# A conditioned residual layer on one core: b2's rows spread by TensorE, six of them behind the first up-projections, and the early loads reordered

## Chip, cores and metric

The kernel runs on one core of a Trainium2 chip. The metric is the device time of one launch in microseconds (us). Engines are named as the profile names them: PE (TensorE), DVE (VectorE), ACT (ScalarE), POOL (GpSimd) and SP (SyncE, which only issues DMAs here).

## What is computed

Each of 128 batches is a tile of 128 x 512 floats with an id (`itok`, 0 to 9 once clamped), which picks one of ten sets of weights.

```python
w1 = W1[language_ids]                       # 512 x 128
w2 = W2[language_ids]                       # 128 x 512
h = relu(einsum('bsh,bha->bsa', x, w1) + b1[language_ids][:, None, :])
adapted = einsum('bsa,bah->bsh', h, w2) + b2[language_ids][:, None, :]
y = x + adapted
normed = (y - mean(y)) * rsqrt(var(y) + 1e-5)          # over the last axis
return x + normed * gamma[language_ids][:, None, :] + beta[language_ids][:, None, :]
```

x and the output are 33.5 MB each, W1 and W2 2.6 MB each; beta, gamma, b2 are ten rows of 512.

## The kernel before

A batch is one tile: its 128 rows lie on the 128 partitions. Four batches make a group, which is one x tile (`xs[g]`, four buffers, 1 MB by one DMA in the loop; the first groups come in halves by `load_part`). The order on each engine is written out by hand: `keep` binds every instruction behind the one before it on its engine, so the order of the Python statements is the order of each queue. Waits between engines are placed by the framework from the data and from the buffers of the pools. A DMA also waits for the eighth DMA before it: there are eight completion semaphores in turn.

The work of one batch b, with its names:

- PE: `transpose_x` (four 128x128 transposes of x into PSUM, pxT), `down` (x times W1, ph: eight matmul records), `up` (hT times W2, py: two records; where `b2_by_matmul(b)` holds, a bf16 matmul with `pick` as weights adds b2's row to py first).
- ACT: `copy_xT` (pxT to SBUF), `relu` (ph to hT, with b1), `square` (sum of squares), for every second batch `deviation` (square root), and `stage_w1` (copies the id's W1 out of a resident copy into the buffer w1s).
- DVE: `residual` (py plus x, or plus r = x + b2, with the row's sum), `scale` (by gamma), `finish` (by the row's rstd, plus o), small statistics in between (`rstd_1` to `rstd_4`).
- POOL: `add_b2` (r = x + b2's spread row, where neither PE nor DVE adds b2) and `add_beta` (o = x + beta's spread row).
- SP: loads of x and the `store` of every second batch.

In iteration i of the loop PE does `transpose_x(i)`, `down(i-1)` and `up(i-2)`, and DVE and ACT finish batch i-3 and what is behind it. py has five PSUM buffers (`p_y`), pxT, ph and the statistics one each (`p_x`, `p_h`, `p_s`), w1s five SBUF buffers (`wp`).

Ahead of the loop the rows of beta, gamma and b2 have to stand on all 128 partitions, because the loop adds them by id. beta and gamma: the rows are split into three bf16 parts (`parts`), and `spread(r)` makes row r by one bf16 matmul with a one-hot `pick` into a py buffer, from which ACT (r % 3 == 1) or DVE copies it to `beta_b` or `gamma_b`. `spread_turn` puts these between the first transposes and downs; there are 20. b2 is loaded as one row into one partition (`b2_row`, inside the w1 tile, which is not yet in use), and POOL spreads it by three `partition_broadcast`. The downs of batches 0 to 3 stand ahead of the loop, and `up(0)`, `up(1)` behind them; `up(2)` and `up(3)` are in iterations 4 and 5.

W1 comes in three ways. For the first FIRST = 8 batches `load_first(b)` loads the id's W1 from DRAM straight into w1s[b]; SP reads the id into a register for that, and each load from the sixth on waits for the `down` that frees its buffer. Batches FIRST to 27 take W1 from `w1e`, a copy loaded by two `load_early` DMAs of 1.25 MB. From batch EARLY = 28 on they take it from `w1`, loaded by four `load_w1` inside the loop.

Of the kernel before, what the change touches and what calls it, by code (L numbers as in the profile page):

```python
# [8 lines left out]
FP = mybir.dt.float32  # L9
# [7 lines left out]
P = 128  # L17
G = 4
EPS = 1e-5
FIRST = 8  # L20
EARLY = 28
U = 2

# [2 lines left out]
def cond_resid_kernel(ctx: ExitStack, tc: tile.TileContext, x, itok, W1, b1, W2, b2, gamma, beta, out):  # L26
# [8 lines left out]
    nc = tc.nc  # L35
    B, S, H = x.shape
    L, _, A = W1.shape
# [7 lines left out]
    def keep(ins):  # L45

        engine = ins.ins.engine
        if engine in last:
            tc.add_manual_dep(ins.ins, last[engine], behind, reason="kept order")
        last[engine] = ins.ins.name  # L50
        return ins

    const = ctx.enter_context(tc.tile_pool(name="const", bufs=1))
    xp = ctx.enter_context(tc.tile_pool(name="xp", bufs=4))
# [7 lines left out]
    p_s = ctx.enter_context(tc.tile_pool(name="p_s", bufs=1, space=PSUM))  # L62
    p_y = ctx.enter_context(tc.tile_pool(name="p_y", bufs=5, space=PSUM))

    xs = {}

    def load_x(g):
        t = xp.tile([P, G, H], FP, tag="x", name=f"x_{g}")
        keep(nc.sync.dma_start(out=t, in_=x[g * G : (g + 1) * G].rearrange("b s h -> s b h")))
        xs[g] = t  # L70

    def xb(b):
        return xs[b // G][:, b % G, :]
# [5 lines left out]
    w1 = const.tile([P, L, KC, A], FP, name="w1")  # L79
# [5 lines left out]
    def load_part(lo, hi):  # L85
        dst = xs[lo // G][:, lo % G : lo % G + hi - lo, :]
        keep(nc.sync.dma_start(out=dst, in_=x[lo:hi].rearrange("b s h -> s b h")))  # L87
# [5 lines left out]
    load_part(0, 2)  # L93
    keep(nc.scalar.dma_start(out=b1r, in_=b1))

    b2_row = w1.rearrange("p l k a -> p (l k a)")[0:1, :]
    keep(nc.scalar.dma_start(out=b2_row, in_=b2.rearrange("(o l) h -> o (l h)", o=1)))

    warm = const.tile([P, 1], FP, name="warm")
    keep(nc.vector.memset(warm, 1.0))  # L100
    keep(nc.scalar.activation(warm, warm, AF.Sqrt))
    def load_w1(k):
        keep(
            nc.sync.dma_start(out=w1[:, :, k, :], in_=W1[:, k * P : (k + 1) * P, :].rearrange("l p a -> p l a"))
        )
# [46 lines left out]
    def load_first(b):  # L152
        w1s[b] = wp.tile([P, KC, A], FP, tag="w1s", name=f"w1s_{b}")
        src = W1[bass.ds(lid(b, ET.SP), 1)].rearrange("o (p k) a -> p (o k a)", k=KC)
        keep(nc.sync.dma_start(out=w1s[b].rearrange("p k a -> p (k a)"), in_=src))  # L155

    def load_w2(lo, hi):
        dst = w2[:, lo * H : hi * H].rearrange("p (l h) -> p l h", l=hi - lo)
        keep(nc.sync.dma_start(out=dst, in_=W2[lo:hi].rearrange("l a h -> a l h")))  # L159

    def load_early(lo, hi):
        dst = w1e[:, lo:hi].rearrange("p l k a -> p l (k a)")
        keep(nc.sync.dma_start(out=dst, in_=W1[lo:hi].rearrange("l (p k) a -> p l (k a)", k=KC)))

    load_w2(0, 2)
    load_first(0)
    load_first(1)
    load_part(2, G)
    load_first(2)
    load_first(3)  # L170
    load_w2(2, 6)
    load_w2(6, L)
    xs[1] = xp.tile([P, G, H], FP, tag="x", name="x_1")
    for b in (G, G + 2):
        load_part(b, b + 2)
        load_first(b)
        load_first(b + 1)
    xs[2] = xp.tile([P, G, H], FP, tag="x", name="x_2")
    load_part(2 * G, 2 * G + 2)
    load_early(0, 5)  # L180
    load_early(5, L)
    load_part(2 * G + 2, 3 * G)

    left = rp.tile([P, H], FP, tag="r", name="left")
    keep(nc.vector.tensor_copy(parts[0:R, :], rows[0:R, :]))
# [13 lines left out]
    beta_b = const.tile([P, L * H], FP, name="beta_b")  # L199
    gamma_b = const.tile([P, L * H], FP, name="gamma_b")  # L200
    b2_b = const.tile([P, L * H], FP, name="b2_b")
    for l in range(0, L, 4):
        span = slice(l * H, min(l + 4, L) * H)
        keep(nc.gpsimd.partition_broadcast(b2_b[:, span], b2_row[:, span]))  # L204

    def spread(r, copier):
        t = (beta_b, gamma_b)[r // L]
        row = p_y.tile([P, H], FP, tag="y", name=f"row_{r}")
        pick_r = pick[:, r : r + 1].to_broadcast([96, P])
        keep(nc.tensor.matmul(row, lhsT=pick_r, rhs=parts[:96, :], start=True, stop=True))  # L210
        dst = t[:, r % L * H : (r % L + 1) * H]
        if copier is nc.scalar:
            keep(nc.scalar.copy(dst, row))
        else:
            keep(nc.vector.tensor_copy(dst, row))  # L215
# [2 lines left out]
    phs, pxs, sums = {}, {}, {}  # L218

    def b2_by_matmul(b):  # L220
        return b < 4 or (b % 4 == 1 and not b2_by_vector(b))

    def b2_by_vector(b):
        return b % 8 == 5 and 8 <= b < B - 16
# [6 lines left out]
    def transpose_x(b):  # L231
        pxs[b] = p_x.tile([P, KC, P], FP, tag="xT", name=f"pxT_{b}")
        for k in range(KC):
            if b < EARLY:
                cols = xb(b).rearrange("s (p k) -> s k p", k=KC)[:, k, :]
            else:
                cols = xb(b)[:, k * P : (k + 1) * P]
            keep(nc.tensor.transpose(pxs[b][:, k, :], cols, ident))  # L238

    def copy_xT(b):  # L240
        xT[b] = tp.tile([P, KC, P], FP, tag="xT", name=f"xT_{b}")
        keep(nc.scalar.copy(xT[b], pxs.pop(b)))  # L242
# [14 lines left out]
    def down(b):  # L257
        phs[b] = p_h.tile([P, P], FP, tag="h", name=f"ph_{b}")
        for k in range(KC):
            keep(  # L260
                nc.tensor.matmul(  # L261
                    phs[b], lhsT=w1s[b][:, k, :], rhs=xT[b][:, k, :], start=(k == 0), stop=(k == KC - 1)
                )
            )
        del xT[b], w1s[b]
# [5 lines left out]
    def up(b):  # L271
        v = lid(b, ET.PE)
        ys[b] = p_y.tile([P, H], FP, tag="y", name=f"py_{b}")
        m = b2_by_matmul(b)
        if m:
            pick_b = pick[:, bass.ds(v + 2 * L, 1)].to_broadcast([96, P])
            keep(nc.tensor.matmul(ys[b], lhsT=pick_b, rhs=parts[:96, :], start=True, stop=False))  # L277
        keep(nc.tensor.matmul(ys[b], lhsT=hT[b], rhs=w2[:, bass.ds(v * H, H)], start=not m, stop=True))  # L278
        del hT[b]
# [78 lines left out]
    def on(b):  # L358
        return 0 <= b < B
# [123 lines left out]
    def spread_turn(lo, hi):  # L483
        for r in range(lo, hi):
            spread(r, nc.scalar if r % 3 == 1 else nc.vector)
# [9 lines left out]
    for b in range(4):  # L495
        down(b)
        if b < 2:
            transpose_x(b + 2)
        relu(b)
        if b < 2:  # L500
            copy_xT(b + 2)
        spread_turn((10, 14, 18, 20)[b], (14, 18, 20, 20)[b])
    up(0)
    up(1)

    for i in range(3, B + U):
        b = i - U - 1
        if b > G and b % G == 2 and b // G + 3 < NG:
            load_x(b // G + 3)
        if i == 5:  # L510
            load_x(3)
        if i in (8, 10, 12, 14):
            load_w1((i - 8) // 2)
        if i == 4:
            up(2)
        if i == 5:
            up(3)
        if i > 3 and on(i):
            transpose_x(i)
        if b <= E:  # L520
            add_b2(b + 2)
            add_beta(b)
        if i > 4 and on(i - 1):
            down(i - 1)
        if i > 3 and on(i):
            copy_xT(i)
        if i > 4 and on(i - 1):
            relu(i - 1)
        if i > 5 and on(i - U):
            up(i - U)  # L530


        g, half = divmod(b, 2)
        p = g - 1
        mine, old = 0 <= p < B // 2, 0 <= p - 1 < B // 2
        if b == E:
            add_b2(b + 3)
            add_beta(b + 1)
            add_b2(b + 4)
            for n in range(b + 2, B):  # L540
                add_beta(n)
        if b > E:
            tail(b)
        elif half == 0:
            if on(b):
                residual(b)
            if mine:
                rstd_1(p)
                scale(2 * p)
            if on(b):  # L550
                negative_mean(b)
            if mine:
                rstd_2(p)
            if old:
                finish(2 * p - 1)
                store(p - 1)
            if mine:
                rstd_3(p)
        else:
            if on(b):  # L560
                residual(b)
            if mine:
                rstd_4(p)
                scale(2 * p + 1)
            if on(b):
                negative_mean(b)
            if mine:
                finish(2 * p)
        if 0 <= b <= E:
            square(b)  # L570
            if half == 1:
                deviation(g)
        if i + 1 >= FIRST and on(i + 1):
            stage_w1(i + 1)

        for n, engine in ((i + 3, ET.Activation), (i - U + 3, ET.PE), (b + 1, ET.DVE), (b + 5, ET.Pool)):
            if on(n):
                lid(n, engine)
# [37 lines left out]
```

## Time and profile before

| what | value |
|---|---|
| median of three runs | 313.11 us (312.94 to 313.24) |
| profiled execution: its own time, and the span of its records | 312.74 us, 311.0 us |
| PE busy | 297.9 us, 96% of the span |
| DVE busy | 294.7 us, 95% |
| POOL busy | 285.4 us, 92% |
| ACT busy | 277.8 us, 89% |
| granted PE clock, mean | 0.989 of full speed |
| HBM read, written | 43.60 MB, 33.55 MB: 248 GB/s over the span |
| chain of work that ended last | PE 83%, DMA 8%, DVE 4% |

The shares of busy time are near each other and say little of which engine sets the pace; the slices of the span and the chain of waits are read for that. A PE record is a pipelined matmul whose end is modelled, so distances between starts are used for PE, not durations. Line numbers are those of this kernel; in the changed one they are a few lines lower.

### The profile page before, as it was taken

What the parts mean: (1) busy time and instruction counts of PE and PEld (TensorE: products, weight loads), DVE (VectorE), ACT (ScalarE), POOL (GpSimd) and SP (SyncE); (2) the same over time, 40 slices, a digit from 0 to 9 for tenths busy, and PEclk for the clock granted to TensorE, in tenths of its full rate; (3) what the DMA queues carried; (4) which work ended last, traced back from release to release, by engine and by line L of the source; (5) the groups of instructions that cost most, each with busy time, mean ns of one, the idle gap of its engine ahead of it and who ended that gap; (6) DMA issues with size and microseconds to landing.
All of it is one profiled execution on the core that took longest, in us unless ns stands there. A gap on an engine that the chain in (4) does not pass through costs nothing.

```text
span 311.0 us, 7063 instructions
## 1 busy us (share of the span) xinstructions
PE 297.9 (96%) x1846; PEld 223.1 (72%) x1846; DVE 294.7 (95%) x941; ACT 277.8 (89%) x710; POOL 285.4 (92%) x237
## 2 busy tenths in 40 slices
PE   8998899999999999999999999999999999999970
PEld 3766677878777777777777777777777777777740
DVE  6845999999999999999999999999999999999995
ACT  2655899999999999999999999999999999999982
POOL 1606999999999999999999999999999999999974
PEclk9999999999999999999999999999999999999995
DMA  6999999876777757677866766577765767773234
GB/s 218 346 387 388 373 368 349 295 263 210 269 271 238 233 192 245 231 237 254 270 245 211 232 201 265 209 266 271 249 227 194 245 233 239 245 270 135 87 154 169
DMA packets 43499, 77.61 MB, mean 250 GB/s; under 512 B 1946, under 2 KB 7077, under 8 KB 43459
## 3 DMA queue, kind: packets, MB, share of 16 engines
q1 hardware_dynamic: 43398, 77.10, 71.8%
q8 instruction: 15, 0.25, 0.3%
q14 instruction: 24, 0.20, 0.2%
q10 hardware_dynamic: 62, 0.07, 0.1%
HBM read 43.60 MB, written 33.55 MB: 248 GB/s over the span
## 4 chain that ended last, share of the span: by engine, by line
PE 83%; DMA 8%; DVE 4%; SPq 1%; issue 1%; ACT 1%; DVEq 1%; POOL 0%; ACTq 0%; POOLq 0%
PE ph L261 33%; PE py L278 32%; PE pxT L238 17%; DMA w1e<-in_L_cond_W_dram 4%; DMA x<-in_x_dram 3%; PE py L277 1%; DVE py L293 1%; DVE py L342 1%; DVE o L351 1%; SPq L155 1%; ACT sq L386 0%; SPq L87 0%; DVEq L611 0%; SPq L159 0%; ACT n L402 0%
## 5 line engine op out<-in xcount | busy, mean ns | idle before, releaser
L255 POOL TENSOR_TENSOR o<-x,beta_b 128x512 f32<-128x512 f32 x128 | 163.2, 1290 | 9.4 <-ACT hT L269 9.4
L261 PE MATMUL ph<-xT,w1s 128*128 128x128 f32 x1024 | 135.5, 275 | 0.0
L278 PE MATMUL py<-w,hT 128*128 x256 | 131.2, 594 | 1.4 <-DVE o L351 1.3
L261 PEld LDWEIGHTS ph<-xT,w1s 128*128 128x128 f32 x1024 | 125.0, 192 | 1.5 <-ACT hT L269 0.8
L248 POOL TENSOR_TENSOR r<-x,b_b 128x512 f32<-128x512 f32 x93 | 120.0, 1291 | 0.0
L238 PEld LDWEIGHTS pxT<-ident,x 128*128 128x128 f32 x512 | 67.4, 154 | 65.4 <-issue 47.3
L342 DVE SCALAR_TENSOR_TENSOR py<-py,nmean,gamma_b 128x512 f32<-128x512 f32 x126 | 93.3, 740 | 0.0
L351 DVE SCALAR_TENSOR_TENSOR o<-py,rstd,o 128x512 f32<-128x512 f32 x122 | 90.7, 744 | 1.4 <-POOL o L255 1.4
L308 ACT ACTIVATE sq<-py,sum 128x512 f32<-128x512 f32 x124 | 84.9, 685 | 4.3 <-DVE py L293 4.3
L238 PE MATMUL pxT<-ident,x 128*128 128x128 f32 x512 | 78.1, 275 | 0.5 <-ACT xT L242 0.5
L242 ACT COPY xT<-pxT 128x512 f32<-128x512 f32 x128 | 75.0, 586 | 1.7 <-PE pxT L238 1.6
L293 DVE SCALAR_TENSOR_TENSOR py<-py,r 128x512 f32<-128x512 f32 x93 | 64.4, 692 | 2.5 <-POOL r L248 1.7
L229 ACT COPY w1s<-w 128x512 f32 x100 | 61.2, 612 | 0.0
L269 ACT ACTIVATE hT<-ph,b1T 128x128 f32<-128x128 f32 x128 | 47.1, 368 | 11.2 <-PE ph L261 7.4
L278 PEld LDWEIGHTS py<-w,hT 128*128 128x128 f32 x256 | 40.4, 192 | 4.7 <-issue 1.7
L293 DVE SCALAR_TENSOR_TENSOR py<-py,x 128x512 f32<-128x512 f32 x35 | 24.3, 695 | 3.3 <-PE py L278 2.7
L308 ACT ACTIVATION_READ_ACCUMULATOR sq<-py,sum 128x1 f32 x124 | 25.2, 203 | 0.0
L319 ACT ACTIVATE sd<-ssq,eps 128x2 f32<-128x2 f32 x62 | 18.3, 296 | 2.1
L299 DVE TENSOR_SCALAR nmean<-sum 128x1 f32<-128x1 f32 x128 | 19.3, 150 | 0.1
L325 DVE RECIPROCAL stat<-sd 128x2 f32<-128x2 f32 x62 | 12.8, 207 | 1.3 <-ACT sd L319 1.3
L204 POOL PARTITION_BROADCAST b_b<-w x3 | 5.6, 1968 | 9.0 <-DVE beta_b L215 9.0
L229 ACT COPY w1s<-w1e 128x512 f32 x20 | 12.2, 612 | 1.3 <-DMA w1e<-in_L_cond_W_dram 1.2
(55 smaller groups left out, 119.7 us busy)
## 6 DMA issues: line engine op xcount, KB each, us to landing
out_dram<-o SPq DMA_DIRECT2D x61, 512.0 KB, 3.6
x<-in_x_dram SPq DMA_DIRECT2D x29, 1024.0 KB, 6.4
x<-in_x_dram SPq DMA_DIRECT2D x6, 512.0 KB, 7.0
w1e<-in_L_cond_W_dram SPq DMA_DIRECT2D x2, 1280.0 KB, 13.4
w<-in_L_cond_W_dram SPq DMA_DIRECT2D x4, 640.0 KB
w1s<-in_L_cond_W_dram SPq DMA_DIRECT2D x8, 256.0 KB, 6.2
w<-in_L_cond_W_dram SPq DMA_DIRECT2D x2, 1024.0 KB
out_dram<-o SPq DMA_DIRECT2D x6, 256.0 KB, 2.0
```

Source lines behind the costliest of these rows:

```text
L229: keep(nc.scalar.copy(w1s[b].rearrange("p k a -> p (k a)"), src))
L238: keep(nc.tensor.transpose(pxs[b][:, k, :], cols, ident))
L242: keep(nc.scalar.copy(xT[b], pxs.pop(b)))
L248: keep(nc.gpsimd.tensor_tensor(rs[b], xb(b), b2_b[:, bass.ds(v * H, H)], ALU.add))
L255: keep(nc.gpsimd.tensor_tensor(os[g][:, j, :], xb(b), beta_b[:, bass.ds(v * H, H)], ALU.add))
L261: nc.tensor.matmul(phs[b], lhsT=w1s[b][:, k, :], rhs=xT[b][:, k, :], start=(k == 0), stop=(k == KC - 1))
L269: keep(nc.scalar.activation(hT[b], phs.pop(b), AF.Relu, bias=b1T[:, bass.ds(lid(b, ET.Activation), 1)]))
L278: keep(nc.tensor.matmul(ys[b], lhsT=hT[b], rhs=w2[:, bass.ds(v * H, H)], start=not m, stop=True))
L293: nc.vector.scalar_tensor_tensor(ys[b], ys[b], 1.0, r, ALU.mult, ALU.add, accum_out=col(sums, b))
L308: nc.scalar.activation(sq, ys[b], AF.Square, bias=col(sums, b), scale=-float(H), accum_out=col(ssqs, b))
L342: nc.vector.scalar_tensor_tensor(ys[b], ys[b], col(nmeans, b), gamma_b[:, bass.ds(v * H, H)], ALU.add, ALU.mult)
L351: nc.vector.scalar_tensor_tensor(o, ys.pop(b), rstds[g][:, j : j + 1], o, ALU.mult, ALU.add)
```

## The change

Four edits go together.

- b2's rows: `b2_row` and the three broadcasts on POOL are gone. `spread` handles rows 20 to 29 (b2) too. Rows 20 to 23 join the turns ahead of the loop, which hold 5, 4, 3 and 2 rows now instead of 4, 4, 2 and 0. The last six, 24 to 29, are `spread_late`: their PSUM tile comes from `p_s`, which has one buffer and is shared with the statistics, and ACT copies them all. They stand behind `up(0)`, `up(1)`, `up(2)`, `transpose_x(4)`, `up(3)` and `down(4)`.
- `b2_by_matmul` holds for b < 6 instead of b < 4; batch 5 was already among them, so batch 4 is the one that moves from POOL to PE.
- FIRST is 12: `load_first` also serves batches 8 to 11, and the first `stage_w1` is that of batch 12. The four `load_w1` go from iterations 8 to 14 to iterations 14 to 20.
- SP's order: W2 is loaded in parts of 4 and 6 ids instead of 2, 4 and 4; x of batches 4 to 11 stands ahead of W1's early copy, whose halves stand around `load_first(10)`, `load_first(11)` and x of batches 12 and 13; x of 12 to 15 comes in halves there and no longer in iteration 5.

```diff
--- before.py
+++ after.py
@@ -17,7 +17,7 @@
 P = 128
 G = 4
 EPS = 1e-5
-FIRST = 8
+FIRST = 12
 EARLY = 28
 U = 2
 
@@ -92,9 +92,6 @@
     keep(nc.scalar.dma_start(out=rows[2 * L : 3 * L, :], in_=b2))
     load_part(0, 2)
     keep(nc.scalar.dma_start(out=b1r, in_=b1))
-
-    b2_row = w1.rearrange("p l k a -> p (l k a)")[0:1, :]
-    keep(nc.scalar.dma_start(out=b2_row, in_=b2.rearrange("(o l) h -> o (l h)", o=1)))
 
     warm = const.tile([P, 1], FP, name="warm")
     keep(nc.vector.memset(warm, 1.0))
@@ -162,24 +159,26 @@
         dst = w1e[:, lo:hi].rearrange("p l k a -> p l (k a)")
         keep(nc.sync.dma_start(out=dst, in_=W1[lo:hi].rearrange("l (p k) a -> p l (k a)", k=KC)))
 
-    load_w2(0, 2)
+    load_w2(0, 4)
     load_first(0)
     load_first(1)
     load_part(2, G)
     load_first(2)
     load_first(3)
-    load_w2(2, 6)
-    load_w2(6, L)
-    xs[1] = xp.tile([P, G, H], FP, tag="x", name="x_1")
-    for b in (G, G + 2):
+    load_w2(4, L)
+    for g in range(1, 4):
+        xs[g] = xp.tile([P, G, H], FP, tag="x", name=f"x_{g}")
+    for b in range(G, 10, 2):
         load_part(b, b + 2)
         load_first(b)
         load_first(b + 1)
-    xs[2] = xp.tile([P, G, H], FP, tag="x", name="x_2")
-    load_part(2 * G, 2 * G + 2)
+    load_part(10, 12)
     load_early(0, 5)
+    load_first(10)
+    load_first(11)
+    load_part(12, 14)
     load_early(5, L)
-    load_part(2 * G + 2, 3 * G)
+    load_part(14, 16)
 
     left = rp.tile([P, H], FP, tag="r", name="left")
     keep(nc.vector.tensor_copy(parts[0:R, :], rows[0:R, :]))
@@ -199,13 +198,10 @@
     beta_b = const.tile([P, L * H], FP, name="beta_b")
     gamma_b = const.tile([P, L * H], FP, name="gamma_b")
     b2_b = const.tile([P, L * H], FP, name="b2_b")
-    for l in range(0, L, 4):
-        span = slice(l * H, min(l + 4, L) * H)
-        keep(nc.gpsimd.partition_broadcast(b2_b[:, span], b2_row[:, span]))
-
-    def spread(r, copier):
-        t = (beta_b, gamma_b)[r // L]
-        row = p_y.tile([P, H], FP, tag="y", name=f"row_{r}")
+
+    def spread(r, copier, late=False):
+        t = (beta_b, gamma_b, b2_b)[r // L]
+        row = (p_s if late else p_y).tile([P, H], FP, tag="s" if late else "y", name=f"row_{r}")
         pick_r = pick[:, r : r + 1].to_broadcast([96, P])
         keep(nc.tensor.matmul(row, lhsT=pick_r, rhs=parts[:96, :], start=True, stop=True))
         dst = t[:, r % L * H : (r % L + 1) * H]
@@ -218,7 +214,7 @@
     phs, pxs, sums = {}, {}, {}
 
     def b2_by_matmul(b):
-        return b < 4 or (b % 4 == 1 and not b2_by_vector(b))
+        return b < 6 or (b % 4 == 1 and not b2_by_vector(b))
 
     def b2_by_vector(b):
         return b % 8 == 5 and 8 <= b < B - 16
@@ -499,29 +495,40 @@
         relu(b)
         if b < 2:
             copy_xT(b + 2)
-        spread_turn((10, 14, 18, 20)[b], (14, 18, 20, 20)[b])
+        spread_turn((10, 15, 19, 22)[b], (15, 19, 22, 24)[b])
+
+
+    def spread_late(r):
+        spread(r, nc.scalar, late=True)
+
     up(0)
+    spread_late(24)
     up(1)
+    spread_late(25)
 
     for i in range(3, B + U):
         b = i - U - 1
         if b > G and b % G == 2 and b // G + 3 < NG:
             load_x(b // G + 3)
-        if i == 5:
-            load_x(3)
-        if i in (8, 10, 12, 14):
-            load_w1((i - 8) // 2)
+        if i in (14, 16, 18, 20):
+            load_w1((i - 14) // 2)
         if i == 4:
             up(2)
+            spread_late(26)
         if i == 5:
             up(3)
+            spread_late(28)
         if i > 3 and on(i):
             transpose_x(i)
+        if i == 4:
+            spread_late(27)
         if b <= E:
             add_b2(b + 2)
             add_beta(b)
         if i > 4 and on(i - 1):
             down(i - 1)
+        if i == 5:
+            spread_late(29)
         if i > 3 and on(i):
             copy_xT(i)
         if i > 4 and on(i - 1):
```

## The prediction

> **What bounds the kernel now.** I read the 40 slices first, to see where the kernel is not full.
>
> ```profile
> PE   8998899999999999999999999999999999999970
> DVE  6845999999999999999999999999999999999995
> POOL 1606999999999999999999999999999999999974
> DMA  6999999876777757677866766577765767773234
> ```
>
> A slice is 7.8 us. From the fifth slice on all four engines stand at nine tenths; only the first four have holes, and there DMA is full. The waits between 48 and 300 us show no engine held for more than 0.4 us. The chain of waits says which of the full engines sets the pace.
>
> ```profile
> 8.18 10.55 DMA x<-in_x_dram
> 18.74 13.36 DMA w1e<-in_L_cond_W_dram
> 32.72 0.59 ACT xT L242
> 33.36 0.74 PE pxT L238 x4
> 34.10 0.89 PE ph L261 x8
> 34.99 0.86 PE py L278 x2
> ```
>
> Columns: start, length, what. After 34 us the chain is PE alone: 0.89 (down) + 0.86 (up) + 0.47 (transposes) = 2.22 us a batch, and 0.22 more where b2 goes by matmul (py L277 at 39.32, L278 at 39.54). The down of batch 8 (ph8) starts at 33.94 and that of batch 12 (ph12) at 43.08. So the end follows the moment at which PE gets into step: **every us by which ph12 moves, the end moves**. Before 34 us the chain is a DMA: SP issued W1's early copy late and it landed at 32.10.
>
> The waits from 5 to 34 us, and POOL's order of time, show who held PE there.
>
> ```profile
> POOL o L255 <- ACT hT L269: 9.4, 1, 9.4
> POOL b_b L204 <- DVE beta_b L215: 9.0, 1, 9.0
> PE py L278 <- DVE o L351: 1.3, 1, 1.3
> ACT w1s L229 <- DMA w1e<-in_L_cond_W_dram: 1.2, 1, 1.2
> PE pxT L238 <- ACT xT L242: 0.5, 1, 0.5
> 10.65 5.64 POOL L204 PARTITION_BROADCAST b_b<-w  x3 [8.95 <-DVE beta_b L215]
> 25.69 2.50 POOL L255 TENSOR_TENSOR o<-x,beta_b 128x512 f32<-128x512 f32 x2 [9.39 <-ACT hT L269]
> ```
>
> POOL stands 9 us ahead of its three broadcasts and 9.4 us behind them. The releasers named are chance: add_beta(0) needs only x and beta_b, done by 11.7. Because o comes at 25.69, finish(0) and finish(1) are late, and with them the PSUM slots of py5 and py6; ACT stands for w1e and PE for xT behind it.
>
> **What the Trainium skill says.** "GPSIMD Engine Reference", 2.1 Instruction dispatch: the first call to freshly loaded GpSimd code pays a load of about 6 us that has no instruction of its own in the profile. The two silent gaps fit, but here they are 9.0 and 9.4 us. "DMA: Bandwidth & Descriptors", Anatomy of one DMA: about 2 us fixed, most of it completion. Here the W2 rest landed at 17.37 (SP's wait for w ends there), 0.8 us after the bandwidth view had summed up to its last byte (4.8 MB), so less shows in a full queue. "Perfetto Trace Analysis", Optimization Strategy: repeated gaps on the engine that should be full can mean too few PSUM buffers for the next tile; before, py5 and py6 wait so, and the change makes a new chain through a single PSUM buffer.
>
> **The change, by parts.**
>
> Removed: b2_row's DMA and POOL's broadcasts with both gaps. POOL can start add_beta at 11.7 and is never late again, so PE's waits for finish go: py5's 0.5 us (27.29 to 27.79) and py6's 1.5 (29.33 + 0.89 = 30.22 to 31.72). One POOL add (b = 4, 1.26 us) turns into a PE matmul of 0.22.
>
> FIRST 12: ACT asks for w1e only after sq of batch 8, so px9's 0.8 us and ph8's 0.1 behind the 32.10 landing go as well. Before, PE's work from py0 (17.46) to ph8 (33.94), 16.48 us, is 7 ups 6.02, 4 pick matmuls 0.88, 6 transposes 2.82, 4 downs 3.56 = 13.28; **3.2 us are waits** (px5 and ph5 0.3, the rest as above).
>
> Added before py0: four rows of b2. Rows leave PE every 0.22 us (four from 13.59, ph2 at 14.45). DVE gets two more copies at 0.62, ACT one at 0.5; both keep up (last row at about 17.4; DVE free for residual 0 by 18.6). Starting from px2 at 10.80 as before and laying 14 rows, 3 downs and px3 end to end: ph1 12.5, ph2 14.7, ph3 16.3, py0 **17.8** instead of 17.46. W2's rest is no later in bytes (4.5 MiB queued up to it in both; estimate 16.7 to 17.4), so it no longer holds py0.
>
> Added after py0: six late rows (24 to 29) and b = 4's pick, 7 x 0.22 = 1.54 us of PE. Their copies are all on ACT, and their PSUM pool has **one** buffer: row n+1 waits for the copy of row n, and the ACT order is sq0, row 26, row 27, xT4, sq1, sd0, row 28, row 29, xT5. Prices, all from before: row start to copy 0.42 (13.59 to 14.01), copy 0.59, next ACT instruction after 0.50 (21.27 to 21.75), sq to sd 0.85, sd to next 0.2, xT's end to the next transpose 0.24 with its weight load (21.86 to 22.10). From py0 = 17.80:
>
> - bm1 18.88, bm2 20.18, row 26 21.26, px4 21.48. Copy 26 from 21.68 to 22.27; row 27 at 22.32 instead of 21.95: wait 0.4.
> - Copy 27 22.74, xT4 23.24 to 23.83, px5 24.07 (PE free at 23.84: 0.2), ph4 24.54.
> - sq1 23.74, sd0 24.6, copy 28 24.8 to 25.4, row 29 25.43, copy 29 25.85, xT5 26.35 to 26.94, px6 27.18. PE was free at 25.65: **wait 1.5**.
> - ph5 27.65, pick and py4 to 29.62, px7, ph6 30.09, pick and py5, px8, ph7 32.53, py6, px9, ph8 34.75. DVE's rstd of batch 0 sits behind copy 29 in the same PSUM buffer (26.5), finish(0) ends near 29.6, before py5's pick at 31.0; finish(1) near 32.0, before py6 at 33.4. No wait.
>
> Sum from py0 to ph8: 13.28 + 1.54 + waits 2.1 = 16.95. So ph8 is at 34.75 against 33.94: +0.34 (py0) + 1.54 (work) - 1.1 (waits 3.2 to 2.1) = +0.8. From there to ph12 three plain batches and one with the pick, 9.10 as before (9.14): ph12 43.85 against 43.08, **+0.8 us**.
>
> SP's queue: load_first(9), (10), (11) each wait for the W1 slot of a down (4, 5, 6), and w1e's second half and the x loads stand behind them. Up to the load for batch 8, 7.7 MB are queued, which the bandwidth view of before reaches at 24 us: DMA runs dry there and starts again at 25.6. From w1s of batch 9 to w1e's second half are 4.46 MB. Before, 4.72 MB took the 13.36 us up to 32.10, 0.353 MB/us; so 12.6 us, landing near 39 to 40.5. ACT needs it at 41.2 (ph10 at 39.2 + 1.1, hT 0.25, sq 0.66). Before, ph8 followed the landing by 1.84; ph12 at 43.85 is touched from a landing at **42.0** on. The cover is 1.5 us or more.
>
> At nothing: store(0) stands behind these loads, but its o slot is next used by add_beta(10), which has about 9 us before finish(10); W1's four loads move to iterations 14 to 20 and are needed at 28 (some 15 us later); x loads keep seven iterations ahead. If DMA stayed full past 60 us, xT of batch 24 would be late next.
>
> The profiled execution: 312.74 with span 311.0, 0.37 under the median 313.11. I add the difference to the median: 313.11 + 0.8 = **313.9**.
>
> **Rivals.**
>
> *The late rows hide (faster).* If ACT gets round to each copy while PE has other work, PE's new waits shrink from 2.1 to about 0.3. Then -3.2 + 1.54 + 0.34 + 0.3 = -1.0: 312.1. It decides from new waits under 0.7 us on. For it: ACT is idle 42% of 5 to 34 us. Against: idle time doesn't help a serial chain of five copies, two squares and a single buffer, whose every length is measured.
>
> *W1's early copy is late again (slower).* SP's waits for downs leave DMA idle, and stores and x behind w1e share the engines. Landing at 43.5 gives ph12 at 45.3: +2.3, 315.4; at 44.5, 316.4. For it: w1e landed 2.0 us after its byte count before. Against: that lag is in the 0.353.
>
> *Nothing to see.* Loss and gain are of one size; 0.5 us less ACT chain or py0 at 17.5 gives +0.3 or less, 313.4.
>
> POOL loading code in spite of the change is excluded: no broadcast is left in its queue.
>
> **How the numbers follow.** A measurement of this kernel tells about 0.2%, 0.63 us, from no change (312.48 to 313.74). Likeliest, +0.8: own range +0.2 to +1.7 (py0 17.5 to 18.3, chain 0.3 either way), 0.54. Late rows hidden, 0.16. Early copy late, 0.14. Nothing to see, 0.16. Of the likeliest about a quarter lies within 0.2% as well, and 0.02 of the hidden case. So faster 0.14, same 0.30, slower 0.56. Range for 8 in 10: 312.2 to 315.6, leaving out the best of the first rival and the worst of the second.
>
> **What would show it.** Right: POOL's first add at about 12 us and no idle after; row 29's copy at about 26 with px6 behind it, PE idle 1.5 us there; ph8 near 34.7; w1e landed by 41 with no ACT wait; 2.22 us a batch after that. Wrong: px6 before 26 (the rows hide); an ACT wait for w1e or for w1s; py0 after 18.5; any PE wait after 45 us.

## The result, and the profile after

| | before | after |
|---|---|---|
| median (lowest to highest), 13 runs each | 313.12 us (312.67 to 314.6) | 314.02 us (313.83 to 314.29) |
| profiled execution: its time, its span | 312.74, 311.0 us | 314.04, 312.3 us |
| down of batch 8 (ph8), of batch 12 (ph12) | 33.94, 43.08 us | 35.49, 44.59 us |
| from ph12 to the end of the span | 267.9 us | 267.7 us |

The ratio is 1.0025 with a 95% interval of 1.0016 to 1.0035: the change costs 0.9 us. The forecast was 313.9. Some executions of the kernel before and of e8 below (34 of 143, and 11 of 22) had a granted clock of 0.982 to 0.987 and took more than 314 us, so e8's median of 313.69 lies between two groups, the lower of them at 312.29 to 313.32.

First the slices of the changed kernel's page (rows 2, each digit a slice of 7.8 us):

```profile
PE   7898999999999999999999999999999999999970
DVE  6774999999999999999999999999999999999995
POOL 1504978999999999999999999999999999999974
DMA  6994999998776657677765767688676767783244
```

From the eighth slice on PE, DVE and POOL stand at nine tenths as before; what has moved lies in the first 55 us. PE is fuller in the fifth slice and emptier in the first two, POOL still has its empty third slice, and DMA, which was full in the fourth, stands at 4 there.

The chain of waits of the changed kernel (start, length, what) shows what ended last on the way to 35 us ("..." marks lines left out):

```profile
4.49 6.86 DMA x<-in_x_dram
11.48 0.72 PE pxT L234 x4
...
18.67 0.86 PE py L274 x2
...
22.55 0.59 ACT b_b L209
23.19 0.38 PE row L206
...
26.86 0.30 ACTq L134
27.16 0.60 ACT xT L238
27.81 0.74 PE pxT L234 x4
```

W1's early copy, which held 13.36 us of the chain before, is gone from it. In its place stand a load of x (batches 2 and 3, asked for at 4.49 and landed at 11.35), a copy of a late b2 row by ACT, and ACT's copy xT of batch 5. The waits from 5 to 36 us of the changed kernel put numbers on them:

```profile
POOL r L244 <- ACT b_b L209: 11.1, 1, 11.1
DVE stat L321 <- ACT b_b L209: 4.2, 1, 4.2
PE pxT L234 <- ACT xT L238: 1.2, 1, 1.2
PE pxT L234 <- DMA x<-in_x_dram: 1.0, 1, 1.0
```

The last two hold PE: 1.0 us at px2 (the transposes of batch 2) and 1.2 us at px6. The first two look large and cost nothing. DVE's reciprocal for batch 0 sits behind copy 29 in the same PSUM buffer and is still early enough. POOL, in its order of time:

```profile
11.31 4.96 POOL L251 TENSOR_TENSOR o<-x,beta_b 128x512 f32<-128x512 f32 x4 [9.85 <-DVE beta_b L211]
27.34 1.28 POOL L244 TENSOR_TENSOR r<-x,b_b 128x512 f32<-128x512 f32 x1 [11.08 <-ACT b_b L209]
```

It makes o for the first four batches at once, then stands until row 29 is copied, since r of batch 6 may be of any id. No PE wait follows from that.

### The profile page after: what moved, and what is told of

Same layout as the page of the kernel before. It is cut to its first block, busy times and chain, and to the rows that moved or that the text cites. A ratio compares the mean times of both kernels' runs of the same rounds, so it can differ in the third digit from the quotient of the medians.

```text
span 312.3 us, 7101 instructions
## 1 busy us (share of the span) xinstructions
PE 298.7 (96%) x1857; PEld 223.6 (72%) x1857; DVE 296.6 (95%) x944; ACT 279.9 (90%) x713; POOL 278.9 (89%) x233
## 4 chain that ended last, share of the span: by engine, by line
PE 88%; DVE 4%; DMA 2%; issue 1%; ACT 1%; DVEq 1%; SPq 0%; POOL 0%; ACTq 0%; POOLq 0%
PE ph L257 35%; PE py L274 33%; PE pxT L234 17%; DMA x<-in_x_dram 2%; PE py L273 2%; PE row L206 1%; DVE py L289 1%; DVE py L338 1%; DVE o L347 1%; ACT sq L382 0%; DVEq L618 0%; SPq L152 0%; ACT n L398 0%; DVE o L409 0%; ACT b_b L209 0%
## 5 line engine op out<-in xcount | busy, mean ns | idle before, releaser
L244 POOL TENSOR_TENSOR r<-x,b_b 128x512 f32<-128x512 f32 x92 | 118.9, 1293 | 13.1 <-ACT b_b L209 11.1
L289 DVE SCALAR_TENSOR_TENSOR py<-py,x 128x512 f32<-128x512 f32 x36 | 25.1, 697 | 2.0 <-PE py L274 0.9
L289 DVE DVE_READ_ACCUMULATOR py<-py,r 128x1 f32 x92 | 13.3, 144 | 0.0
L333 DVE RECIPROCAL rstd<-stat 128x2 f32<-128x2 f32 x62 | 10.4, 168 | 0.0
```

The lines of the kernel that those rows point to most:

```text
L244: keep(nc.gpsimd.tensor_tensor(rs[b], xb(b), b2_b[:, bass.ds(v * H, H)], ALU.add))
L289: nc.vector.scalar_tensor_tensor(ys[b], ys[b], 1.0, r, ALU.mult, ALU.add, accum_out=col(sums, b))
```

## The experiments

Beside the ten edited kernels the kernel before was timed again: its median was 312.94 beside e1 to e4, 312.93 beside e5 to e8 and 312.77 beside e9 and e10. The median of before was 313.12 beside the changed kernel, so medians of different series are set against their own before. The ratios in the table lie nearer to those of the means, 0.03 to 0.18% under those of the medians. Short names: **rows** is b2 spread by TensorE, six rows late, and b < 6 in `b2_by_matmul`; **loads** is SP's new order with FIRST = 12; **split** is W2 in parts of 2, 4 and 4 ids again. px2 is the transposes of batch 2, py0 the first up. The dates are those of one profiled execution each; a wait and its releaser stand in brackets.

| kernel | px2 (wait) | py0 | ph8 | ph12 | span | median | ratio to before |
|---|---|---|---|---|---|---|---|
| before | 10.80 | 17.46 | 33.94 | 43.08 | 311.0 | 313.12 | |
| before, second trace | 11.38 (0.52, hT) | 18.01 | 34.04 | 43.18 | 311.1 | | |
| after = rows + loads | 11.48 (0.96, x) | 18.51 | 35.49 | 44.59 | 312.3 | 314.02 | 1.0025 [1.0016, 1.0035] |
| rows + loads + split (e1) | 10.42 | 17.37 | 34.35 | 43.45 | 311.6 | 313.33 | 0.9994 [0.9975, 1.0013] |
| the same, x first (e9) | 11.15 | 18.10 | 35.09 | 44.19 | 312.3 | 313.42 | 1.0011 [0.9997, 1.0024] |
| after, late copies by DVE (e2) | 11.54 (0.97, x) | 18.57 | 34.91 | 44.01 | 311.7 | 313.46 | 1.0007 [0.9990, 1.0024] |
| e1 + e2 (e5) | 11.00 | 17.95 | 34.14 | 43.24 | 311.4 | 312.55 | 0.9985 [0.9973, 0.9998] |
| rows alone (e3) | 10.75 | 17.70 | 34.84 | 43.94 | 311.9 | 313.05 | 0.9995 [0.9982, 1.0008] |
| rows alone, second trace (e12) | 10.14 | 17.09 | 34.07 | 43.17 | 311.1 | | |
| loads alone (e4) | 12.19 (0.98, x) | 18.57 | 33.88 | 42.98 | 311.1 | 312.64 | 0.9978 [0.9962, 0.9994] |
| loads + split (e7) | 10.83 (0.54, hT) | 17.91 | 32.88 | 41.98 | 310.1 | 311.81 | 0.9956 [0.9933, 0.9978] |
| o of 0 and 1 by DVE, alone (e8) | 11.32 (0.97, x) | 17.96 | 34.33 | 43.47 | 311.4 | 313.69 | 1.0013 [0.9996, 1.0030] |
| loads + split + that (e6) | 10.29 | 17.38 | 31.20 | 40.61 | 308.7 | 311.07 | 0.9935 [0.9918, 0.9953] |
| the same, x first (e10) | 10.51 | 17.37 | 31.19 | 40.55 | 308.7 | 310.58 | 0.9917 [0.9893, 0.9942] |

One thing is to be read off the whole table first: span minus ph12 lies between 267.7 and 268.2 us in all 14 traces. The end follows ph12, so a shift of PE's dates ahead of 45 us can stand for a shift of the time of that execution.

**W2 in three parts again (e1).**

```diff
-    load_w2(0, 4)
+    load_w2(0, 2)
...
-    load_w2(4, L)
+    load_w2(2, 6)
+    load_w2(6, L)
```

> The changed kernel with W2 loaded in parts of 2, 4 and 4 ids again, all else as changed. Theory: x of batches 2 and 3 landed near 11.4 us only because W2's first part is 0.5 MiB longer, and PE waited 0.96 us for it before px2; with the short part px2 is near 10.8 and py0 near 17.8 instead of 18.5, everything behind moves by 0.6 to 0.7 us, and the time is 313.4 (ratio to before 1.000 to 1.002). Rival: py0 then waits for the last part of W2 (17.4 before) or PE meets its rows' copies instead, and less than 0.2 us is won: 313.9. In both px6 still stands 1.2 to 1.5 us behind xT5.

Measured 313.33: 0.4 over the median of before beside it, where the changed kernel is 0.9 over its own. The ratios, 0.9994 and 1.0025, are further apart, and their intervals don't touch. PE's order of time, e1:

```profile
10.42 0.64 PE L235 MATMUL pxT<-ident,x 128*128 128x128 f32 x4
26.66 0.75 PE L235 MATMUL pxT<-ident,x 128*128 128x128 f32 x4 [1.16 <-ACT xT L239]
```

px2's wait for x is gone, px6's is as it was, and all dates from py0 on are 1.14 us earlier. So the wait for x came with the half MiB that the longer first W2 part puts ahead of x. The other traces agree: px2 waits for x in all three with the long part (0.96 to 0.98 us), in one of the nine with the short part ahead of x (e8, below), and in neither of the two with x first.

**Late rows copied by DVE (e2).** Rows 27 to 29 leave ACT.

```diff
-        spread(r, nc.scalar, late=True)
+        spread(r, nc.vector if r > 26 else nc.scalar, late=True)
```

> The changed kernel with the copies of the late rows 27, 28 and 29 on DVE instead of ACT. Theory: the serial chain of row copies, xT4, squares and xT5 on ACT makes PE wait for px6; DVE is idle from 23.0 to 27.3 us there, so with three copies on it px6 comes 1.1 us earlier (near 26.7), ph8 near 34.5 instead of 35.5, and the time falls by 1.0 us to 313.0. Rival: the wait only moves, because DVE's copies hold back residual and finish, and py5 or py6 waits for a PSUM slot: less than 0.3 us won, 313.8.

px6 came at 26.75 with no wait, 1.06 earlier, as expected. ph8 and ph12 gained only 0.58, and the time 0.4 (313.46, 0.5 over its before) instead of the expected 1.0; the intervals of the two ratios overlap, so the gain in time isn't clear of the noise. ACT's order of time, e2, shows where the rest went:

```profile
25.05 0.69 ACT L304 ACTIVATE sq<-py,sum 128x512 f32<-128x512 f32 x1 [1.32 <-DVE py L289]
28.07 0.69 ACT L304 ACTIVATE sq<-py,sum 128x512 f32<-128x512 f32 x1 [1.11 <-DVE py L289]
```

DVE copies rows where it had made residuals, so ACT waits for the residuals, and PE loses 0.20 and 0.27 us in the next two batches (from ph5 to ph6 2.64 us and to ph7 2.71, instead of 2.44 each). Half of the gain in the trace was given back.

**Rows alone (e3) and loads alone (e4).** e3 takes FIRST = 8, SP's order, the place of `load_x(3)` and the iterations of `load_w1` from before; e4 takes these four from after and leaves b2 to POOL, with b < 4.

```diff
# e3, against after
-FIRST = 12
+FIRST = 8
...
-    load_w2(0, 4)
+    load_w2(0, 2)
...
-        if i in (14, 16, 18, 20):
-            load_w1((i - 14) // 2)
+        if i == 5:
+            load_x(3)
+        if i in (8, 10, 12, 14):
+            load_w1((i - 8) // 2)
```

> b2's rows by PE and batch 4's pick as changed, but FIRST 8, SP's order and the times of W1's loads as before. Theory: with the rows on PE, ph8 comes near 34.8 us whatever W1's early copy does (it lands at 32.1 and ACT asks for it at about 32 to 33), so FIRST 12 brings nothing beside them; and W2's first part is short again, which wins the 0.7 us of px2. So 313.4, 0.6 faster than the changed kernel. Rival: FIRST 12 is worth the 0.9 us that PE lost behind w1e before, and without it the rows alone give 0.9 us more than changed, less the 0.7 of px2: 314.2 or later, with ACT waiting for w1e by 1 us or more.

> b2 by POOL's broadcasts as before (batch 4 too), but FIRST 12 and SP's order as changed. Theory: POOL's first add stays near 25.7 us and py5 and py6 wait for finish as before, 2.0 us together, but px9 and ph8 no longer wait behind w1e, 0.9 us; no row is added on PE. ph8 near 33.1, and 312.3 to 312.4: 0.7 to 0.9 us faster than before, 1.6 faster than changed. Rival: the late start of SP's loads (DMA idle from 20 us on) or x of batches 2 and 3 landing at 11.4 takes the 0.9 us away: 313.1 or more.

Rows alone cost nothing that can be told (313.05, 0.35 less than expected), loads alone gain 0.1% by the medians and 0.2% by the ratio (312.64, a little less than expected, with ph8 at 33.88 instead of 33.1), and together they lose 0.25%. The second trace of e3 below says why the loads bring nothing beside the rows. With rows, PE comes to batch 8 too late to meet W1's early copy at all; ACT's order of time of that trace, with FIRST = 8:

```profile
31.46 0.62 ACT L223 COPY w1s<-w1e 128x512 f32 x1
```

There is no wait in brackets: the same copy had waited 1.2 us before. The wait that FIRST = 12 takes away is not there any more, so of the loads only their price is left, px2's wait. In e4 the loads do pay: no wait for w1e, but px2 at 12.19 behind x, and py6 then waits 1.31 for finish, which stands behind POOL.

**Both repairs (e5)**: e1 and e2 in one.

> The changed kernel with both edits of the first two experiments: W2 in parts of 2, 4 and 4 ids, and the copies of late rows 27, 28 and 29 on DVE. Theory: the two costs lie in different places (x of batches 2 and 3 before py0; the chain of copies after it), so they add: 0.7 and 0.5 us less than changed, 312.7 to 312.9, level with the kernel before; the ten rows themselves (2.4 us of PE work with batch 4's pick) are what is left. Rival: the second only showed because PE was late anyway; then it is the 313.3 of the first alone.

Measured 312.55, a little better than expected. The two repairs add up as far as the noise lets one tell: set against before, e5 is 1.3 us under the changed kernel, by the medians and by the ratios; the two alone make 0.5 and 0.4 us by the medians, 1.0 and 0.6 by the ratios.

**What the rows were to remove, removed at its source.** The trace of before had PE waiting for what POOL made late: o of batches 0 and 1, and r of batch 4, for which DVE waited 1.72 us with finish(1) behind it. The two adds of o can go to DVE, which has room there, batch 4's b2 can go to PE as in the change, and POOL can keep its broadcasts. e6 does both with the changed loads and the split, e7 has these loads without it, e8 is the two edits alone on the kernel before.

```diff
# e8, against before; e6 has it too
-        return b < 4 or (b % 4 == 1 and not b2_by_vector(b))
+        return b < 6 or (b % 4 == 1 and not b2_by_vector(b))
...
-        v = lid(b, ET.Pool)
-        keep(nc.gpsimd.tensor_tensor(os[g][:, j, :], xb(b), beta_b[:, bass.ds(v * H, H)], ALU.add))
+        engine, queue = (ET.DVE, nc.vector) if b < 2 else (ET.Pool, nc.gpsimd)
+        v = lid(b, engine)
+        keep(queue.tensor_tensor(os[g][:, j, :], xb(b), beta_b[:, bass.ds(v * H, H)], ALU.add))
```

> The loads as changed (FIRST 12, SP's order) with W2 in parts of 2, 4 and 4; b2's rows by POOL's broadcasts as before, so no row is added on PE; the o of batches 0 and 1 is added by DVE instead of POOL, and batch 4's b2 by PE's pick. Theory: all that PE lost before in the start was finish(0), finish(1) and r of batch 4 waiting for POOL, which stands until 25.7 us, and W1's early copy. Both are gone here at a cost of 0.22 us of PE, so ph8 comes near 31.1 us instead of 33.9 and ph12 near 40.2, unless w1e lands after 38.4; the time is 310.2, 2.7 us faster than before, or up to 311.0 if w1e is a little late. Rival: something else on POOL (o of batches 2 and 3, r of batch 6) holds finish next and less than 1 us is won: 312.

> The loads of the changed kernel alone, b2 as before, with W2 in parts of 2, 4 and 4 ids. Theory: without the 1 us that PE waited for x of batches 2 and 3, the gain of FIRST 12 shows whole: ph12 near 42.1, 0.9 us before that of the kernel before, 312.0; py5 and py6 still wait 2.0 us for finish. Rival: the shift is eaten by these waits, because finish(1) hangs on POOL's 25.7 and not on PE: then 312.6 as without the split.

> The kernel before with two edits: o of batches 0 and 1 by DVE, and batch 4's b2 by PE's pick; FIRST 8 and the loads as before. Theory: the two delays of the start lie beside each other: without POOL's, PE and ACT simply wait for W1's early copy (landing 32.1), ACT's wait grows from 1.2 to over 3 us, ph8 stays at 33.9 and the time at 312.9, within 0.2% of before. Rival: they lie one behind the other, and 2 us are won: 311.

e7 came as expected (311.81), e6 at the upper end of what was expected (311.07), and e8 has no gain (313.69; its lower group has a median of 312.7, where 312.9 was expected). e8 shows that the two delays, POOL's late work and the late landing of W1's early copy, lie beside each other in time, each covering the other. ACT's order of time, e8:

```profile
32.59 0.62 ACT L229 COPY w1s<-w1e 128x512 f32 x1 [3.34 <-DMA w1e<-in_L_cond_W_dram]
```

and PE's:

```profile
33.75 0.75 PE L238 MATMUL pxT<-ident,x 128*128 128x128 f32 x4 [2.27 <-ACT xT L242]
```

With o in time, ACT comes to w1e 2 us sooner and simply waits longer; ph8 is at 34.33, no earlier than before (33.94 and 34.04). Without the wait for w1e alone (e7) it is at 32.88, without both (e6) at 31.20. e6 and e7 differ by 1.7 us at ph8 and by 0.7 in their medians. Part of that difference is lost again: in e6 ACT waits 1.10 us for w1e after all, now for batch 12, and from ph8 to ph12 PE takes 9.41 us, where e7 takes 9.10.

e8 also has a wait for x at px2, though its loads are those of before. So x can be late with the short first W2 part as well. In e8 DMA moved only 260 GB/s from 6 to 8 us and 239 from 8 to 10, where e1 has 396 and 355; why is left open.

**x ahead of W2 (e9 on e1, e10 on e6).**

```diff
+    load_part(2, G)
     load_w2(0, 2)
     load_first(0)
     load_first(1)
-    load_part(2, G)
     load_first(2)
```

> The changed kernel, W2 in parts of 2, 4 and 4 ids again, and x of batches 2 and 3 asked for ahead of the first of them. Theory (px2 waits because x stands behind the first W2 part in the DMA queue): px2 at 10.4 to 10.5 with no wait for x, as with the split alone, ph12 at 43.3 to 43.5, median 313.1 to 313.3. If executions in which x comes late are also why the split kernel's times spread from 313.05 to 313.93, the upper ones thin out and the median comes nearer to 313.1. Rival (it was the splitting of W2, not the place of x): ph0 or py0 gets a new wait in place of px2's, since W1 of batch 0 has the same 1 MiB ahead of it as in the changed kernel and W2's first part comes later: py0 at 17.8 or later, 313.6 or more.

> The kernel with b2 by POOL, beta of batches 0 and 1 by DVE and the changed loads with W2 in three parts, x of batches 2 and 3 asked for ahead of W2. In its trace px2 had no wait at 10.29, so nothing is to be gained in a good execution: ph12 at 40.5 to 40.7, median 310.9 to 311.1. Rival (x is late in a good part of its executions): median 310.6 or less. If W2's first part is then late for py0, py0 moves past 17.4: 311.4 or more.

px2 waits for x in neither. But e9's median is 313.42, not the expected 313.1 to 313.3. The upper times did thin out: 13 of 14 lie between 313.12 and 313.58, where e1 has four of 14 above 313.6. Whether late x is what spreads e1's times is left open. The one high run of e9, 314.07, is the profiled one, and its trace shows another source: DVE waited 1.31 us for the rows of b2 (0.31 in e1), the first spread row came at 6.91 instead of 5.89, and py0 is 0.73 later than in e1 with no wait between. e5, with e1's loads, has that wait too (1.15 us), so x first does not explain it. e10 is the best version measured, 310.58 in six runs; its profile has ph12 where e6 had it (40.55 and 40.61), and the two intervals overlap, so that x first helps there isn't shown. e10 and e6 beat both kernels. PE waits briefly for W2 in e10:

```profile
17.37 1.10 PE L282 MATMUL py<-w,hT 128*128 x2 [0.39 <-DMA w<-in_L_cond_W_dram]
```

**The kernel before and rows alone, a second trace each (e11, e12).**

> The kernel before, unchanged, for a second trace. Theory (the end follows ph12): the time from ph12 to the end is again 267.7 to 268.1 us, and ph12 at 43.1 plus whatever the time is over 312.74. Rival: px2 waits for x in some executions of this kernel too (1 us); or the executions above 314 us, which have a lower clock, lose their time after ph12.

> The kernel with b2's rows by TensorE and the loads of before, unchanged, for a second trace: the first was profiled at 313.70 where its median is 313.05. Theory (the end follows ph12): ph12 at 43.94 less what its time is under 313.70, so near 43.3 for a time of 313.05, and the missing 0.65 us lies ahead of ph12, in px6's wait or in the ups behind it. Rival: ph12 at 43.9 again and a shorter way from there to the end.

e11 took 312.83: py0 at 18.01, 0.55 later than in the first trace, and ph8 at 34.04, only 0.10 later. PE's order of time, e11:

```profile
31.63 1.12 PE L278 MATMUL py<-w,hT 128*128 x2 [1.18 <-DVE o L351]
33.46 0.74 PE L238 MATMUL pxT<-ident,x 128*128 128x128 f32 x4 [0.70 <-ACT xT L242]
```

The time from ph12 to the end is 267.9 us again, as expected. The waits for o and w1e took up what came late ahead of them: in these two traces of before, py0 is not on the path. e12 took 312.88, 0.82 less than the first trace of rows alone, and ph12 is 0.77 earlier. Of the expectation, the date is right and the place is wrong: nothing is different in px6's wait or the ups. py0 is 0.61 earlier, and 0.16 lies between py0 and ph8. With rows the waits that took up a late start are gone, and a late start goes to the end in full.

## Why the prediction was right, and where it was not

**The way from py0 to ph8.** Predicted 16.95 us as 13.28 of work, 1.54 added and 2.1 of new waits; measured 16.98 in the changed kernel, and 16.98, 16.98 and 16.99 in e1, e12 and e9 (17.14 in e3). The wait at px6, forecast as 1.5, is 1.3 by the distance of PE's starts; the rest of the 2.1 is in small pieces, as at row 27. The single-buffer chain on ACT, seen from py0: px5 at +6.27 predicted and +6.34 measured, row 29 at +7.63 and +7.76, px6 at +9.38 and +9.30. ACT's order of time, changed kernel:

```profile
25.65 0.57 ACT L209 COPY b_b<-row 128x512 f32<-128x512 f32 x1
26.68 0.59 ACT L209 COPY b_b<-row 128x512 f32<-128x512 f32 x1 [0.46 <-PE row L206]
27.16 0.59 ACT L238 COPY xT<-pxT 128x512 f32<-128x512 f32 x1
```

Copy 29 waits for its matmul, the matmul had waited for copy 28, and xT5 stands behind both: that is the one PSUM buffer that the prediction named with the Trainium skill, "Perfetto Trace Analysis", Optimization Strategy. Unlike the repeating gap that the section tells of, it is a single gap of 1.2 us at px6; e2, which took three copies off that chain, removed it.

**From px2 to py0.** Predicted 7.0 us (10.80 to 17.80), measured 7.03 in the changed kernel and 6.95 in e1, e3, e5, e9 and e12, against 6.66 and 6.63 in the two traces of before. So the rows cost the 0.3 us here that was forecast.

**The term that was mis-sized: the start, "+0.34 (py0)".** It measured +1.05 in the profiled pair. PE's order of time, px2 and py0, before and changed:

```profile
10.80 0.72 PE L238 MATMUL pxT<-ident,x 128*128 128x128 f32 x4
17.46 1.10 PE L278 MATMUL py<-w,hT 128*128 x2
```

```profile
11.48 0.72 PE L234 MATMUL pxT<-ident,x 128*128 128x128 f32 x4 [0.96 <-DMA x<-in_x_dram]
18.51 1.02 PE L274 MATMUL py<-w,hT 128*128 x2
```

The length was right; "Starting from px2 at 10.80 as before" was wrong. px2 started at 11.48, behind x; without that wait it would have been 10.52. The prediction worked out when W2's rest would land ("no later in bytes") but not what the longer first W2 part does to the x load queued behind it, so it never priced that edit at px2. py0 came at 18.51 and ph8 0.7 later than forecast; "py0 after 18.5" stood among the signs that it was wrong, and it was this step. The date of px2 also moves by itself: it was 10.80 and 11.38 in the two traces of before, and 10.14 to 11.15 in the kernels with rows and no wait for x. One pair of traces is a weak base for a start of a few tenths; the medians of the changed kernel and e1 bear the wait out.

**Why 313.9 came out all the same.** Up to ph12 the profiled pair moved 1.51, not 0.8. It moved 0.2 less behind it, and the profiled execution of before lay 0.38 under its median while that of after lay at its own (314.04 and 314.02). 1.51 - 0.2 - 0.4 is 0.9. So the sign and the mechanism behind py0 were right, and the closeness of the median to 313.9 is partly luck: one term too small by 0.7, against 0.6 that lies in the choice of traces and behind ph12.

**The other steps.** The slices were read one too early: PE's and ACT's fifth stands at eight tenths before, and nine hold from the sixth on; no term rests on it. The waits of py5 and py6 for finish are gone, and ACT does not wait for w1e (it makes w1s of batch 12 at 41.96 without one): right. From ph8 to ph12 9.10, predicted 9.10. After 36 us no PE matmul waits: right. POOL's first add at 11.31, predicted about 12: right; "no idle after" was wrong by the 11.1 us up to 27.34, at no cost. The two silent stretches that the prediction read with the Trainium skill, "GPSIMD Engine Reference", 2.1 Instruction dispatch, as a code load are there in every kernel that keeps the broadcasts (8.4 to 9.8 us ahead of them, 8.9 to 9.5 behind). In the kernels with b2 by TensorE POOL stands about as long, but for an operand: 9.9 us for beta_b in the changed one, and then it adds at once. This fits a load, if a longer one than the page's 6 us; no run took the load apart from the broadcast.

That DMA would run dry behind SP's waits for downs was right: from 24 to 27 us it moved 16 GB/s at most, and it started again after 27, not at 25.6. Busy time by stretch, changed kernel (after the engines: granted clock, DMA share, GB/s):

```profile
20.00:25.00 5.00, 4.78 (x18) 2.01 (x17) 2.21 (x8) 3.63 (x8) 0.00 (x0) 1.00 0.72 263
25.00:30.00 5.00, 3.84 (x29) 3.11 (x28) 2.67 (x11) 4.13 (x12) 2.66 (x3) 1.00 0.57 159
```

SP's own waits name the cause, the loads of w1s:

```profile
SPq L152 <- PE row L206: 10.1, 3, 7.8
SPq L152 <- PE ph L257: 6.9, 4, 2.6
```

(That PE's row is named as releaser is chance; these loads wait for downs.) W1's early copy did not hold PE, but that its cover was the forecast 1.5 us isn't shown. ACT takes it at 41.96 without a wait; but in e2, with the same loads, ACT stood 0.65 us ahead of that copy with no releaser named, in e5, whose loads differ by the split alone, it waited 0.30 us for it, and in e6, where PE is 4 us earlier, 1.10.

**The rivals.** That the late rows hide did not happen: PE's new wait at px6 was 1.2 us. That W1's early copy is late again did not happen in the changed kernel. "Nothing to see" is what rows alone came to (0.9995). The prediction took before's waits of 3.2 us as a fixed credit for the whole change. e11 shows that they are slack: with a later py0 they shrink (the way from py0 to ph8 is 16.03 there, not 16.48), so such a sum of terms need not hold for another execution.

## What to carry to other kernels

Two delays that lie beside each other in time hide each other: here removing one alone gives nothing (e8), the other about 0.4% (e7), both about 0.6% (e6). Two edits that each remove the same stretch of idle time don't add, while their prices do: loads with the split gain that 0.4% alone and nothing beside the rows. When a load is made longer to bring one operand sooner, follow what is queued behind it up to its first use; and ask whether the late work can be moved at its source (two small adds to an engine with room) before ten rows are re-routed.

## What the hardware showed that I had not expected

- One program starts at different dates: the first down of rows alone came at 9.25 us in one execution (e12) and 9.85 in another (e3), and with the same loads DVE waited 0.31 us for the rows of b2 in e1 and 1.15 in e5. The kernel with slack behind its start swallowed such a shift (before: 0.55 us at py0 became 0.10 at ph8); the one without passed it on (rows alone: 0.61 at py0 became 0.77 at ph12).
- The changed kernel's 13 runs lie within 0.5 us, while rows alone spread over 0.95. That px2's wait for x evens the start out is a guess: px2 came at 11.48 and 11.54 in the two traces with rows and the long first W2 part, but at 12.19 in e4.
- In the three kernels with the long first W2 part DMA moved 256 to 282 GB/s from 4 to 6 us, in all others 359 to 387. That may have made x later still, beside the half MiB itself; the cause was not found.
- With the same loads queued, DMA moved between 239 and 366 GB/s from 8 to 10 us (e8 and before). The cause was not found.
